# Grouped expert FFN: token parts of 8 (or 20 and 12) in place of 12 and 20, one slot array of 144 tiles, and slot tiles between the routing of later parts

## The chip, the cores and the metric

The kernel runs on one core of a Trainium2 chip. The metric is the device time of one execution in microseconds; lower is better. TensorE (PE) does the matrix products, VectorE (DVE) and ScalarE (ACT) the elementwise work, GpSimd (POOL) issues the indirect DMAs, SyncE (SP) the plain ones. All data are float32.

## The reference

The input is 8 sequences of 512 tokens with 256 features, 4096 token rows in all. Two layers run one after the other, each with a half-weighted FFN, an attention and another half-weighted FFN, and each of these reads a layer-normalized x:

```python
x = x + 0.5 * L0_ffn(LN(x))      # 8 experts, each takes its top k tokens
x = x + L0_attn(LN(x))           # rope, causal, 16 heads of 16
x = x + 0.5 * L0_ffn(LN(x))
x = x + 0.5 * L1_ffn(LN(x))      # mixture of experts, the first one
x = x + L1_attn(LN(x))           # 16 heads of 64; adds its input as well
x = x + 0.5 * L1_ffn(LN(x))      # the second one
```

The change concerns `L1_ffn`. Each token chooses 4 of 16 experts:

```python
scores = softmax(x @ gate_w.T)                  # 16 experts in 4 groups of 4
masked = scores of the 2 groups with the largest maximum, 0 elsewhere
weights, indices = top_k(masked, 4)
a = silu(x @ w1[e]) * (x @ w3[e])               # 256 -> 128, for each chosen e
y = sum over the chosen e of weight * (a @ w2[e])
z = (silu(x @ ws1) * (x @ ws3)) @ ws2           # shared expert, 256 -> 256 -> 256
return y + z
```

## The kernel before

**Stages.** x stays in SBUF as 32 token tiles of 128 rows. In the profiled execution the stages follow each other like this: first FFN of layer 0 (`ffn0(0)`) to about 660 us, its attention (`attn0`) to 1466, `ffn0(1)` to 2116, the first mixture-of-experts stage (`ffn1_before`) to 2670, the attention of layer 1 (`attn1`) to 3979, and the second mixture-of-experts stage (`ffn1_after`) to the end at 4489.

**Slots.** The mixture of experts is grouped. A token row goes to DRAM four times, once for each of its experts, into rows ("slots") ordered by expert, so that each slot tile of 128 rows belongs to one expert; the tiles are then multiplied by that expert's weights, and the results are gathered back. `Grouped` holds this for one stage. The 32 token tiles are cut into two parts, `PARTS = 12, 20`; the first stage takes them as (12, 20), the second as (20, 12). Each part has its own slot arrays in DRAM, `slots_d[t]` for the inputs and `ys_d[t]` for the outputs. Every expert's rows are rounded up to whole tiles, so that a part of t token tiles needs

```python
return (t * P * TOPK + E1 * (P - 1)) // P      # 63 for t = 12, 95 for t = 20
```

slot tiles, 158 for a stage, whatever the tokens choose. Slots that no token takes must hold finite numbers; `clear` (L133 to L135) writes zeros to `slots_d`, 20.2 MB in 16 DMAs on SP, from inside the expert loop of `ffn0(0)`.

**Steps of a part.**
- *Rows and logits.* Statistics (bn at L157 and L158, finish at L165 to L173), normalized rows (`rows`, L1212), transposes (`columns`, L1409 and L1412), router products (`logits`, L1417) into a PSUM tile `lg` that holds the part's token tiles.
- *Routing* (`routing`, L1244 to L1321). A generator of short groups of DVE operations, advanced from outside: softmax, four rounds of top-k (L1177 to L1188), a prefix sum over the tokens by expert with two matmuls (`pp`, L1282 and L1290), the slot number of each choice (`pick`, `where`, L1305 to L1309), the expert of each slot tile (`owner`, L1317), the weights of the choices (`coef`).
- *Sends* (`send`, L1221). Four indirect DMAs for each token tile, issued on POOL. A manual dependency keeps two of them in flight.
- *Slot tiles* (`tile_steps`). For each group of four tiles a load `xs` (L1488, on SP; it waits for all sends of its part) and a store `ys` (L1538). One tile is: transposes `tpx` (L1500), a `value_load` of the expert's number on PE (L1503), four matmuls `hs` (L1510), silu and product (L1516, L1518), transpose `tpa` (L1522), two matmuls `yps` (L1530). The stages of five successive tiles are interleaved in one `step`.
- *Collecting* (`collect`). One step adds the four results of token tile t-2 to x (L1341, DVE) and issues four gathers of token tile t (L1328, POOL), into two `yg` buffers.

**Order.** In both stages the order on PE, DVE, ACT, POOL and SP is the program's (`manual_schedule` with these engines); in `ffn0` SP is not in that list, in `attn0` neither POOL nor SP. The shared expert is cut into units of PE work with the DVE work that follows; `Pump` issues the PE part of the next unit and then the DVE part of the last one (hidden L1438 to L1449, outputs L1460 and L1466).

In `ffn1_before` all preparation comes ahead of the slot tiles: rows and routing of part 0, its sends, rows, logits and routing of part 1, its sends, with shared units between; then 158 tiles in one row. From tile 69 on, every sixth step is followed by one collecting step of part 0. `attn1` takes the collecting steps of part 1 over, 22 of them, one with each second half-chunk, prepares the first part of the second stage on the side (`Front`: rows on POOL, router products, `routing(0)`), and sends its rows (`front.send`). In `ffn1_after` the tiles of part 0 (20 token tiles) start at once, the routing of part 1 is advanced by two with every step, and its sends follow. After the last tile comes the shared expert of all 32 token tiles, with the remaining collecting steps between the units; each token tile is stored when its collected rows and its shared outputs are in (L1743).

Of the kernel before, what the change touches and what calls it, by code (L numbers as in the profile page):

```python
# [46 lines left out]
PARTS = 12, 20  # L47
# [9 lines left out]


def slot_tiles(t):

    return (t * P * TOPK + E1 * (P - 1)) // P


class Kernel:
    def __init__(self, ctx, tc, w):
# [59 lines left out]
        self.slots_d, self.ys_d = {}, {}  # L125
        for t in PARTS:
            self.slots_d[t] = self.dram.tile([slot_tiles(t) * P, D], F32, name=f"slots_d{t}")
            self.ys_d[t] = self.dram.tile([slot_tiles(t) * P, D], F32, name=f"ys_d{t}")

    def clear(self, zero, part, parts):  # L130

        for t in PARTS:
            rows = self.slots_d[t].rearrange("(j p) d -> p j d", p=P)  # L133
            a, b = slot_tiles(t) * part // parts, slot_tiles(t) * (part + 1) // parts
            self.nc.sync.dma_start(out=rows[:, a:b, :], in_=bc(zero, 1, b - a))  # L135
# [69 lines left out]
    def _ffn0(self, ctx, n, beside):  # L205
# [272 lines left out]
        if n == 0:  # L478
            zero = pool.tile([P, D], F32, name="zero")
            nc.gpsimd.memset(zero, 0.0)  # L480
# [5 lines left out]
        for e in range(E0):  # L486
# [4 lines left out]
            if n == 0:  # L491
                self.clear(zero, e, E0)
# [40 lines left out]
    def _attn0(self, ctx, weights):  # L533
# [330 lines left out]
        with tc.manual_schedule(engines={E.PE, E.DVE, E.Activation}):  # L864
# [22 lines left out]
            for g in range(G):  # L887
                n, kt = divmod(g, QT)
                b, half = divmod(g // 8, 2)
                if g % 8 == 0:  # L890
                    units = (first_half, second_half)[half](b)
                    if half == 1 and b + 2 < B:
                        normal(b + 2)()
                if g < 8:
# [39 lines left out]
    def _attn1(self, ctx, weights, beside, after):  # L934
# [172 lines left out]
        steps = after.routing(0, front.lg, front.pool, row_psum)  # L1107
# [14 lines left out]
        with tc.manual_schedule(engines={mybir.EngineType.PE, mybir.EngineType.Pool}):  # L1122
# [5 lines left out]
            for n in range(N):  # L1128
# [10 lines left out]
                for half in range(2):  # L1139
# [6 lines left out]
                    if half == 0 and n > 0 and beside:  # L1146
                        beside.pop(0)(behind)
# [43 lines left out]
class Grouped:  # L1191


    def __init__(self, k, n, parts):
        self.k, self.n, self.parts = k, n, parts
        self.base = (0, parts[0])
        self.tiles = [slot_tiles(t) for t in parts]
        self.slots_d = [k.slots_d[t] for t in parts]
        self.ys_d = [k.ys_d[t] for t in parts]
        late, most = k.late, max(parts)  # L1200

        self.slot = [late.tile([P, TOPK, most], I32, name=f"slot{h}", bufs=2) for h in range(2)]
        self.coef = [late.tile([P, TOPK, most], F32, name=f"coef{h}", bufs=2) for h in range(2)]

        self.owner = [late.tile([1, slot_tiles(most)], I32, name=f"owner{h}") for h in range(2)]
        self.stats = k.ln_tiles(late)
        self.sent, self.of_part = [], ([], [])
        self.got, self.y = [], {}

# [6 lines left out]
    def send(self, h, t, row):  # L1216

        nc, tc = self.k.nc, self.k.tc
        key = f"slots{self.n}{h}"
        for r in range(TOPK):  # L1220
            inst = nc.gpsimd.indirect_dma_start(  # L1221
                out=self.slots_d[h][:, :],
                out_offset=bass.IndirectOffsetOnAxis(ap=self.slot[h][:, r, t : t + 1], axis=0),
                in_=row, in_offset=None,
                bounds_check=self.tiles[h] * P - 1, oob_is_err=True,
# [4 lines left out]
            tc.declare_no_dep(inst, group=key, keep=before, reason="slots of one part are all different")  # L1230
            tc.add_to_no_dep_group(key, inst)
# [3 lines left out]
    def routing(self, h, lg, pool, row_psum):  # L1235
# [40 lines left out]

# [6 lines left out]
        inc = pool.tile([P, E1, HT], F32, name=f"left{E1}")  # L1283
        nc.vector.tensor_tensor_scan(inc.rearrange(flat), carry.rearrange(flat), pb, 0.0, ALU.mult, ALU.add)
        tiles_i = pool.tile([P, E1], I32, name="tiles_i")
        nc.vector.tensor_scalar(tiles_i, inc[:, :, HT - 1], float(P - 1), None, ALU.add)
        nc.vector.tensor_scalar(tiles_i, tiles_i, 7, None, ALU.arith_shift_right)
        nc.vector.tensor_tensor(inc.rearrange(flat), inc.rearrange(flat), pb, ALU.subtract)
        pa = row_psum(E1 * HT)
        nc.tensor.matmul(pa, lhsT=k.tri, rhs=chosen.rearrange(flat), start=True, stop=True)  # L1290
        tiles = pool.tile([P, E1], F32, name="tiles")
        nc.vector.tensor_copy(tiles, tiles_i)
        upto = pool.tile([P, E1], F32, name="upto")
        nc.vector.tensor_tensor_scan(upto, k.ones[:, 0:E1], tiles, 0.0, ALU.mult, ALU.add)
        base = pool.tile([P, E1], F32, name="base")
        nc.vector.tensor_tensor(base, upto, tiles, ALU.subtract)
        nc.vector.tensor_scalar(base, base, float(P), None, ALU.mult)
        nc.vector.tensor_tensor(inc.rearrange(flat), inc.rearrange(flat), pa, ALU.add)
        yield
        nc.vector.tensor_tensor(inc, inc, bc(base, 2, HT), ALU.add)  # L1300
        yield
        where = pool.tile([P, TOPK, HT], F32, name="where")
        for r in range(0, TOPK, 2):
            pick = pool.tile([P, 2, HT, E1], F32, name="pick")
            nc.vector.tensor_tensor(  # L1305
                pick, hots[:, r : r + 2], bc(inc.rearrange("p e t -> p t e"), 1, 2), ALU.mult
            )
            nc.vector.tensor_reduce(where[:, r : r + 2], pick, AX.X, ALU.add)
        nc.vector.tensor_copy(self.slot[h][:, :, :HT], where)  # L1309
        yield  # L1310

        past = pool.tile([P, E1], F32, name="past")
        number = pool.tile([P, 1], F32, name="number")
        nc.vector.tensor_scalar(past, upto, k.lanes[:, 0:1], None, ALU.is_le, ALU.add, accum_out=number)  # L1314
# [265 lines left out]
def ffn1_before(k, f):  # L1580
# [3 lines left out]
    with ExitStack() as ctx, k.tc.manual_schedule(engines={E.PE, E.DVE, E.Activation, E.Pool, E.SP}):  # L1584
# [76 lines left out]
        for late in coming:  # L1661
            late()
# [220 lines left out]
```

## Time and profile before

| | |
|---|---|
| time, median of 3 runs | 4433.28 us (4429.19 to 4433.55) |
| the profiled execution: time, span | 4490.85 us, 4489.1 us |
| mean granted TensorE clock in it | 0.918 of full |
| PE busy | 3938.8 us, 88% of the span |
| DVE, ACT, POOL busy | 1951.8, 1451.5, 1224.7 us |
| first mixture-of-experts stage | 2116 to 2670 us; first slot tile's `hs` at 2318.4, last `yps` at 2669.3 |
| second one | 3979 to 4489 us; slot tiles from 4000.5 to 4354.2 |
| slot tiles in both stages | 316 |
| sends (L1221) of the first stage | 48 from 2177.7 to 2243, 80 from 2289.5 to 2440 |

The profile comes from one execution, whose time stands in the table beside its span; the median comes from other executions of the same kernel. Rows of stretches give the busy time of each engine between two points of the span, the number of instructions in brackets, the granted clock of TensorE as a share of full speed, the mean busy share of the 16 DMA engines and what they moved. Rows of a chain give start, length, engine, output tile and line of what the end waited for. Rows of a line give the shortest, median and longest duration in ns, and the first and last start.

### The profile page before, as it was taken

The numbers are of one execution on the slowest core, as the hardware profiler recorded it, in microseconds if no ns is written. First come the engines' busy times: TensorE is split into PE (matmuls) and PEld (weight loads), VectorE is DVE, ScalarE is ACT, GpSimd is POOL, SyncE is SP. The second block draws the span as 40 slices with busy tenths as digits, with TensorE's granted clock in tenths as the row PEclk, the third lists the DMA queues.
The fourth block names the chain that finished last, engine by engine and source line by source line (L and its number), as shares of the span: only waits on it lengthen the run. The fifth ranks groups of instructions, "written<-read, shape, count | busy, mean of one in ns | idle before, by whom it ended". The sixth has DMA issues, their size and how long they took to land.

```text
span 4489.1 us, 52262 instructions
## 1 busy us (share of the span) xinstructions
PE 3938.8 (88%) x17900; PEld 2336.3 (52%) x17900; DVE 1951.8 (43%) x4992; ACT 1451.5 (32%) x3289; POOL 1224.7 (27%) x1133
## 2 busy tenths in 40 slices
PE   5799988999999579998679889999999999989987
PEld 5466653333334556665446654545554554556654
DVE  5221115545454422111443445666555455454454
ACT  2122222433343212222113324454445434433321
POOL 2323323333230132332433212231000112524145
PEclk9999997989896589999789999999999999989998
DMA  8423320000000322332325530010000000135443
GB/s 276 139 58 65 72 58 19 15 20 13 22 22 3 95 55 56 66 72 61 114 81 181 182 116 24 24 33 15 1 1 1 1 1 20 57 116 177 150 149 106
DMA packets 253715, 306.99 MB, mean 68 GB/s; under 512 B 31888, under 2 KB 223504, under 8 KB 253200
## 3 DMA queue, kind: packets, MB, share of 16 engines
q1 hardware_dynamic: 204304, 202.42, 14.7%
q0 software_dynamic: 49152, 101.24, 9.3%
q8 instruction: 148, 2.42, 0.2%
q14 instruction: 111, 0.91, 0.1%
HBM read 161.48 MB, written 133.69 MB: 66 GB/s over the span
## 4 chain that ended last, share of the span: by engine, by line
PE 58%; DVE 11%; issue 6%; ACT 5%; DMA 2%; another core or an unknown queue 1%; POOL 1%; SPq 0%; DVEq 0%; ACTq 0%; POOLq 0%
PE hs L1510 7%; PE pq L1001 5%; PE zp L1061 5%; PE sp L1027 5%; PE op L464 5%; PE hp L453 4%; PE tp L1048 4%; PE st L775 3%; PE yp L1091 3%; PE pv L982 2%; PE pp L643 2%; PE hp L1438 2%; PE yps L1530 2%; ACT ex L1036 1%; DVE x L1341 1%
## 5 line engine op out<-in xcount | busy, mean ns | idle before, releaser
L1036 ACT ACTIVATE ex<-sp,nmax 128x512 f32<-128x512 f32 x512 | 347.4, 689 | 415.7 <-DVE nmax L1033 381.8
L464 PE MATMUL op<-w,hid 128*128 128x256 f32 x2048 | 473.2, 394 | 0.0
L453 PE MATMUL hp<-exT,w 128*128 128x512 f32 x1024 | 448.4, 596 | 0.0
L464 PEld LDWEIGHTS op<-w,hid 128*128 128x128 f32 x2048 | 405.9, 199 | 66.9 <-issue 8.6
L1510 PE MATMUL hs<-w_sb,xT 128*128 x1264 | 363.1, 411 | 74.1 <-DVE xT L195 59.2
L1328 POOL DMA_INDIRECT yg<-ys_d,slot x256 | 262.5, 1025 | 599.5 <-DVE x L1341 249.8
L471 POOL DMA_INDIRECT acc_d<-ob,idx x128 | 199.7, 1560 | 693.4 <-ACT ob L470 396.4
L469 DVE TENSOR_TENSOR ob<-op,b 128x256 f32<-128x256 f32 x128 | 54.4, 425 | 663.7 <-PE op L464 573.7
L1033 DVE TENSOR_REDUCE nmax<-sp 128x2 f32<-128x1024 f32 x256 | 303.3, 1217 | 72.1 <-PE sp L1027 70.6
L1510 PEld LDWEIGHTS hs<-w_sb,xT 128*128 128x128 f32 x1264 | 221.7, 193 | 204.7 <-DVE xT L195 115.8
L1048 PEld LDWEIGHTS tp<-ident,ex 128*128 128x128 f32 x2048 | 227.3, 141 | 190.8 <-issue 129.0
L453 PEld LDWEIGHTS hp<-exT,w 128*128 128x128 f32 x1024 | 194.8, 192 | 232.8 <-issue 231.9
L1048 PE MATMUL tp<-ident,ex 128*128 128x128 f32 x2048 | 275.7, 278 | 36.4 <-ACT eT L193 35.9
L746 DVE CUSTOM_DVE_ANT_0 junk<-sp,mask 128x128 f32<-128x128 f32 (+3 forms) x512 | 248.4, 485 | 126.1 <-PE sp L739 106.6
L457 ACT ACTIVATE hid<-hp,b 128x512 f32<-128x512 f32 x256 | 175.9, 687 | 343.4 <-PE hp L453 340.3
L1027 PE MATMUL sp<-qk,qk 64*128 64x512 f32 x1024 | 262.9, 633 | 1.9 <-ACT ex L1036 1.9
L1221 POOL DMA_INDIRECT slots_d<-wide,slot x176 | 173.7, 987 | 331.7 <-DVE past L1314 125.5
L1001 PE MATMUL pq<-xnT,wide 128*128 128x512 f32 x512 | 252.4, 616 | 6.3 <-DVE eT L195 5.6
L784 ACT ACTIVATE ex<-st 128x1024 f32<-128x1024 f32 (+3 forms) x256 | 174.0, 703 | 239.3 <-DVE st L782 239.0
L1518 DVE TENSOR_TENSOR as<-sgs,hs 128x128 f32<-128x128 f32 x316 | 90.5, 286 | 363.3 <-ACT sgs L1516 330.4
L1061 PE MATMUL zp<-eT,v 128*64 128x512 f32 x1024 | 235.8, 602 | 0.3 <-DVE eT L195 0.3
L470 ACT ACTIVATE ob<-ob,gate 128x256 f32<-128x256 f32 x128 | 65.0, 508 | 510.3 <-DVE ob L469 480.0
(293 smaller groups left out, 6087.2 us busy)
## 6 DMA issues: line engine op xcount, KB each, us to landing
xs<-slots_d SPq DMA_DIRECT2D x76, 512.0 KB
ys_d<-ys SPq DMA_DIRECT2D x76, 512.0 KB
w<-in_W SPq DMA_DIRECT2D x32, 1024.0 KB
w_sb<-in_w SPq DMA_DIRECT2D x24, 512.0 KB
slots_d<-zero SPq DMA_DIRECT2D x7, 1536.0 KB
xn_d<-xn SPq DMA_DIRECT2D x16, 512.0 KB
acc_d<-x SPq DMA_DIRECT2D x8, 1024.0 KB
x<-acc_d SPq DMA_DIRECT2D x16, 512.0 KB
```

The costliest lines, as they stand in the source:

```text
L453: nc.tensor.matmul(hp, lhsT=w1[:, c, f * P : f * P + P], rhs=exT[e][:, c, h * CH : h * CH + CH], start=(c == 0), stop=(c == DC - 1),)
L464: nc.tensor.matmul(op, lhsT=hid[h][:, f, i * P : i * P + P], rhs=w2[:, f, :], start=(f == 0), stop=(f == FC - 1),)
L471: nc.gpsimd.indirect_dma_start(out=acc_d[:, :], out_offset=bass.IndirectOffsetOnAxis(ap=idx[:, e, st : st + 1], axis=0), in_=ob, in_offset ...
L746: nc.vector.tensor_tensor_reduce(out=junk[:, :wd], in0=sps[h // 2][:, h % 2, :wd], in1=mask[:, S - wd :], scale=1.0, scalar=NEG, op0=ALU.a ...
L1001: nc.tensor.matmul(pp, lhsT=(wq, wk)[a][:, k, c * P : c * P + P], rhs=seq[b]["xnT"][:, k, :], start=(k == 0), stop=(k == DC - 1),)
L1027: nc.tensor.matmul(sp[:, j, :], lhsT=q[r, qt * P : qt * P + P], rhs=k[r, :], start=True, stop=True)
L1033: latest[0] = nc.vector.tensor_reduce(nmax, sp, AX.X, ALU.max, negate=True).ins
L1036: nc.scalar.activation(ex[:, j, :], sp[:, j, :], AF.Exp, bias=nmax[:, j : j + 1], accum_out=ch["sums"][:, qt, j : j + 1],)
L1048: nc.tensor.transpose(tp[:, k, :], ch["ex", qt][:, j, k * P : k * P + P], self.ident)
L1061: nc.tensor.matmul(zp[DK1 * j : DK1 * j + DK1, :], lhsT=seq[b]["v", h][:, k, at : at + DK1], rhs=ch["eT"][:, j, k, :], start=(k == 0), sto ...
L1328: inst = nc.gpsimd.indirect_dma_start(out=y[:, r, :], out_offset=None, in_=self.ys_d[h][:, :], in_offset=bass.IndirectOffsetOnAxis(ap=self ...
L1510: nc.tensor.matmul(hp.rearrange("p a i -> p (a i)"), lhsT=st[j]["xT"][:, c, :], rhs=self.w13[:, bass.ds(st[j]["e"], 1), c, :].rearrange("p ...
```

## The change

The slots of a stage now lie in one array for all parts, `SLOTS = FULL + E1 = 128 + 16 = 144` tiles, with one `slots_d` and one `ys_d` in DRAM. Of each expert's rows in a part, as many as fill whole tiles take tiles numbered upwards from the last part's end. What is left over goes to shared tiles, one for each expert at first, numbered downwards from 143, which later parts go on filling; when one is full, the next one downwards is begun. `routing` carries this from part to part in `free`, `rest`, `ends` and `ended`. Tiles from 128 up have a fixed expert (`SLOTS - 1 - number`), so PE loads no number for them.

The constructor works out an order of tiles that holds for any choice of the tokens: `closed[h]` tiles can be computed once the parts before h are sent, and after `ready[h]` tiles everything of part h is computed. For four parts of 8 token tiles `closed` is [0, 17, 33, 49] and `ready` [65, 96, 144, 144]; for parts of 20 and 12, [0, 65] and [96, 144].

```diff
-PARTS = 12, 20
+FULL = TT * TOPK
+SLOTS = FULL + E1
...
     def clear(self, zero, part, parts):
-        for t in PARTS:
-            rows = self.slots_d[t].rearrange("(j p) d -> p j d", p=P)
-            a, b = slot_tiles(t) * part // parts, slot_tiles(t) * (part + 1) // parts
+        a, b = SLOTS * part // parts, SLOTS * (part + 1) // parts
+        for rows in (self.slots_d, self.ys_d):
+            rows = rows.rearrange("(j p) d -> p j d", p=P)
             self.nc.sync.dma_start(out=rows[:, a:b, :], in_=bc(zero, 1, b - a))
...
-            if n == 0:
-                self.clear(zero, e, E0)
...
+                if g >= 16 and g % 8 == 0 and g < 16 + 8 * B:
+                    self.clear(mask[:, 0:D], g // 8 - 2, B)
```

The last two hunks are in the expert loop of `ffn0` and in the step loop of `attn0`; `ys_d` is now cleared too, 37.7 MB together.

In `routing` the rounding to whole tiles gives way to the split into whole tiles and left-over rows; the new operations work mostly on 16 numbers a partition, a few on all (128 for 8 token tiles). `then()` stands for the sends of the part, which are now issued as soon as `slot` is written:

```diff
+        nc.vector.tensor_scalar(over_i, count, P - 1, None, ALU.bitwise_and)
+        nc.vector.tensor_scalar(count, count, 7, None, ALU.arith_shift_right)
+        nc.vector.tensor_copy(tiles, count)
+        nc.vector.tensor_copy(over, over_i)
...
+        full = small("full")
+        first = 0.0 if h == 0 else self.ends[:, 0:1]
+        nc.vector.tensor_tensor_scan(full, k.ones[:, 0:E1], tiles, first, ALU.mult, ALU.add)
...
+        if h > 0:
+            limit, jump, more, other = small("limit2"), small("jump2"), small("more"), small("other")
+            nc.vector.tensor_tensor(limit, jumps[0][0], self.free, ALU.add)
+            nc.vector.tensor_tensor(more, over, self.free, ALU.is_ge)
...
+            jumps.append((limit, jump))
+            yield
+        beyond = [pool.tile([P, E1, HT], F32, name=x) for x in ("masked", "score2")[: len(jumps)]]
+        for b, (limit, jump) in zip(beyond, jumps):
+            nc.vector.tensor_tensor(b, at, bc(limit, 2, HT), ALU.is_ge)
+            nc.vector.tensor_tensor(b, b, bc(jump, 2, HT), ALU.mult)
...
-        nc.vector.tensor_copy(self.slot[h][:, :, :HT], where)
+        nc.vector.tensor_copy(self.slot[:, :, ts], where)
+        then()
```

The rows, columns, logits (now copied from a PSUM tile of four token tiles to SBUF) and the routing of part h are one generator, `front(h)`. `ffn1_before` becomes:

```diff
+        part = f.front(0)
+        while 0 not in f.lg:
+            advance(part, 1)
+        advance(part, 4)
+        pump.feed(groups[0][0] + groups[1][0] + groups[0][1])
+        while advance(part, 3):
             pump.run(1)
...
+        part = f.front(2)
+        while 2 not in f.lg:
+            advance(part, 3)
+            pump.run(1)
+        advance(part, 4)
+        pump.feed(groups[2][1] + groups[4][0])
+        tiles(f.closed[1], part, 3)
...
+        part = f.front(3)
+        pump.feed(groups[3][1] + groups[5][0] + groups[4][1])
+        tiles(f.closed[2], part, 3)
...
+        tiles(f.closed[3], iter(()), 1)
         while pump.units or pump.pending:
             pump.run(1)
-        coming = f.collect(0, 2)
-        begin, weights = f.tiles[0] + 6, None
-        for i in range(total):
+        coming = f.collect(2)
+        begin, weights = f.ready[0] + 6, None
+        for i in range(at, total):
             step(i)
...
-            if i >= begin and (i - begin) % 6 == 0 and coming:
+            if i >= begin and len(coming) > (TT + 2 - f.base[2]) * TOPK:
                 coming.pop(0)()
```

`tiles(until, work, each)` issues one `step` and then advances `work` by `each`. So tiles 0 to 16 run beside the routing of part 2, tiles 17 to 32 beside the rows and routing of part 3, tiles 33 to 48 after it, the other 95 behind the last shared units.

Collecting goes in quarter steps: one add of token tile t-2 and one gather of token tile t for one of the four choices. In the first stage one quarter step follows each tile from tile 71 on; 72 quarter steps are left to `attn1`, which takes four at a time. In `ffn1_after` one or two of them follow each tile from tile 102 on, now with four gathers in flight from the start, and three, three, one, one, one, one follow the shared units after the tiles. Loads of `xs` now wait for the sends of their own and all earlier parts, gathers for the stores of the tiles up to `ready` of their part. A group of loads has at most four tiles and does not reach across a `ready` mark; one group has a single tile.

## The prediction

> **What bounds the kernel now.** I read the head of the page first, then busy time by stretches for the two mixture-of-experts (MoE) stages that the diff rewrites (2116 to 2670 us and 3979 to 4489 us), then the chain of waits inside them, then single lines of code.
>
> ```profile
> PE 3938.8 (88%) x17900; PEld 2336.3 (52%) x17900; DVE 1951.8 (43%) x4992; ACT 1451.5 (32%) x3289; POOL 1224.7 (27%) x1133
> PE   5799988999999579998679889999999999989987
> PEclk9999997989896589999789999999999999989998
> ```
>
> PE is busy 88% of the span, so overall there is little to win except by doing less on PE or by closing the dips. The first MoE stage is digits 19 to 24 of the second and third rows, the second one the last five. The stretches show where its dips are:
>
> ```profile
> core 0: us, PE busy (x) PEld busy (x) DVE busy (x) ACT busy (x) POOL busy (x), PEclk, DMA share, GB/s
> 2142.00:2181.00 39.00, 32.11 (x71) 15.13 (x71) 26.89 (x80) 6.98 (x10) 2.64 (x3) 0.79 0.36 98
> 2181.00:2250.00 69.00, 37.17 (x171) 28.67 (x169) 23.66 (x83) 10.66 (x17) 44.49 (x46) 0.73 0.27 103
> 2250.00:2316.00 66.00, 54.05 (x150) 29.87 (x151) 43.69 (x96) 6.53 (x10) 19.30 (x19) 0.89 0.09 36
> 2316.00:2344.00 28.00, 18.21 (x70) 12.52 (x69) 6.43 (x20) 5.17 (x18) 17.68 (x19) 0.82 0.36 120
> 2344.00:2470.00 126.00, 116.51 (x553) 83.21 (x554) 46.34 (x154) 44.32 (x153) 44.17 (x45) 1.00 0.58 183
> ```
>
> The row of 2344 is the goal: slot tiles back to back, PE busy for 116.5 of 126 us at full granted clock. Everything from 2142 to 2316 is preparation: routing of part 0, rows of part 1, routing of part 1, with the shared expert as the only filler. PE is busy 123 of 174 us there, at a clock of 0.73 to 0.89. No slot tile runs before 2318. One tile's price is read in the chain of waits:
>
> ```profile
> 2460.98 1.15 PE hs L1510 x4
> ...
> 2471.28 1.13 PE hs L1510 x4
> ...
> 2473.50 10.88 DMA xs<-slots_d
> ```
>
> From 2460.98 to 2471.28 are five tiles: 2.06 us each (2.04 over 2344 to 2352). Then the tiles of part 0 are over and PE waits 10.9 us for part 1's rows. The second MoE stage has tiles from 4000.5 to 4354.2 (158, 2.24 us each, with routing or collecting between them), then a tail without tiles:
>
> ```profile
> 4214.00:4354.00 140.00, 117.64 (x557) 84.10 (x557) 70.00 (x208) 45.39 (x156) 58.14 (x58) 1.00 0.52 163
> 4354.00:4404.00 50.00, 38.83 (x99) 20.61 (x98) 20.55 (x44) 5.41 (x10) 32.78 (x31) 0.83 0.33 94
> 4404.00:4489.00 85.00, 61.39 (x200) 36.30 (x198) 38.47 (x82) 9.86 (x17) 41.22 (x40) 0.90 0.38 113
> ```
>
> ```profile
> 4369.39 2.95 DMA yg<-ys_d,slot
> 4372.43 0.49 DVE x L1341
> 4373.08 0.67 POOL yg L1328
> ```
>
> The tail's chain goes round POOL gather, transfer, DVE add, next gather: 71 gathers and 76 adds in 131 us, about 1.8 us per gather. PE has about 100 us of work there.
>
> **The change part by part.**
>
> *Fewer tiles.* 158 slot tiles become 144 in each MoE stage. Fourteen tiles by 2.05 us is 29 us less in each, and it is on the path, since tiles follow each other on PE. In the second stage 16 shared tiles also lose their value_load; 0 to 4 us, taken as 0, since the row of 2344 already has PE 92% busy.
>
> *First stage, order of work.* A timeline. Logits of 8 rather than 12 token tiles: from 2142 to about 2138. Routing of 12 token tiles takes 23.4 us of DVE in 70 instructions, of 20 tiles 32.7 us; the line through both gives 18.7 us for 8. The diff adds 14 small operations to the first routing (about 3 us at 0.2 us) and some 26 to each later one, part of them on all 128 elements (5 to 6 us). All routing together grows from 56 to about 95 us of DVE. That is the change's main price. Part 0's slots are then known at about 2166 (2176.7 before); rows and logits of part 1 until 2190; its routing until 2227; rows of part 2 until 2246, all with shared-expert units on PE. Then 17 whole tiles run beside part 2's routing: 24 us of routing plus 17 by 0.75 us of the tiles' own DVE work is 37 us of DVE in short dependent steps, so I put a step at 3.0 us instead of 2.05: until 2298. Shared units, 10 us. Sixteen tiles beside part 3's rows and routing: 9.5 (1.18 us a token tile, from the 23.66 us of 20 in the row of 2181) +24+12 = 46 us of DVE, 3.6 us a step: 2366. Shared units 14 us (2380), 16 tiles at 2.05 (2413), the last shared units 25 us (2438). The remaining 95 tiles carry 64 quarter steps of collecting; before, a tile with a quarter step cost 2.3 us (2.24 in the second stage with routing), so 95 by 2.05 plus 64 by 0.25 is 211 us: 2649. If the interleaved steps cost only 2.3 us, as the second stage's mixed steps do at their cheapest, 33 us less: 2616. I take 2634, nearer the dear end, because DVE has twice the routing work; 36 us before the 2670 of now. Check from below: 144 tiles, 82 us of shared units (3.44 and 0.86 us each), 36 us of transposes and logits, 22 us until the first logits and 16 of collecting add to 450 us, so 2566 is the floor.
>
> *The sends.* Now 128 row transfers go out from inside the routing (L1221), beside tiles. Their instructions:
>
> ```profile
> L1221 POOL DMA_INDIRECT slots_d<-wide,slot x48: 975/979/1032, 2177.7 to 2242.4; - x48
> ...
> L1221 POOL DMA_INDIRECT slots_d<-wide,slot x45: 974/979/988, 2340.2 to 2438.9; - x45
> ```
>
> The first row has no slot tiles beside it (1.35 us a send), the second has tile loads and stores (2.2 us a send, two in flight). 32 sends at 2.1 us are 67 us: part 0 done at 2230, part 1 at 2290, part 2 by 2355, part 3 from 2364 to 2431. Each is there before its tiles are due, with 0 to 15 us to spare (part 3's at 2438). Here a rule speaks against the change: the Trainium skill, "SBUF — State Buffer", section "SBUF: two separate sides", says that a POOL-issued DMA cannot have its descriptors written while VectorE holds the port they share (620 ns becoming 3100 ns there), so sends inside DVE-heavy routing should slow. The trace says otherwise for these shapes: 974 to 988 ns with DVE at 46 of 126 us, 979 median beside the 24 of 69 us. At the trace's price sends stay hidden; if each of the 96 sends beside routing cost 2.5 us more, 240 us of POOL would make part 3 arrive over 150 us late and take all the gain. I follow the trace.
>
> *Wait at 2473.* Its 10.9 us go if part 3 is in time; late next would be the end of the sends at 2431. This is within the timeline.
>
> *Clearing.* ffn0(0) loses 20.2 MB of DMA writes; the DMA share was 1.05 there, and from indices ready to first hidden matmul took 18.3 us against 14.5 in ffn0(1): 4 us less. The second array adds 16.8 MB more: 37.7 MB now issued on SP in attn0 at every eighth step, 16 transfers. At the 335 to 357 GB/s of the first stage that is about 107 us of DMA; attn0's own traffic there is 0.12 of the share. A pair (4.7 MB, 14 us) delays q and k loads queued behind it on SP by 14 us, while these are asked for 6 to 8 steps (42 to 48 us) ahead. So 0, between 0 and +80.
>
> *attn1.* It takes over 72 quarter steps (18 whole ones) instead of 22 whole: 4 by 4 adds of 0.48 us is 8 us of DVE less, 3 us more routing, on an engine 57% busy under a PE of 96% (2700 to 3950 us): 0, within 5 either way.
>
> *Second stage.* 29 us less for tiles; routing of 12 token tiles 5 us longer, in steps of 2.2 to 3.3 us: +5; a group of one tile and rows that arrive about when due: +2. Sum −22. In the tail 65 gathers are left instead of 71, at 1.8 us each 11 us less, in quarter steps with four in flight rather than in fours; PE's 100 us stand below. I take −12 (between −30 and +10, since the chain shows 9.5 us of bare issue at 4437 there, which no row explains).
>
> Sum: −4 +0 −36 +0 −22 −12 = −74 us. The profiled execution is 4490.85 us (span 4489.1, 1.75 around it), 1.3% above the median 4433.28; 4417/4490.85 of the median is 4360. Its own range: 4330 to 4390.
>
> **The rivals.**
> - *All hidden* (0.15): interleaved tiles cost 2.05 to 2.3, the tail falls by 25. First stage −58, second −27−25, −4: −114, so 4320. For it: DVE is 43% busy. Against: routing is a dependent chain of 0.5 us operations in one in-order queue with the tiles' evictions.
> - *Sends bound the end* (0.22): at 2.3 us each the 128 sends run from 2166 without a break and end at 2461; the last 95 tiles stand until then, 2461+211 = 2672, and the first stage gains nothing: −4−22−12, 4395. For it: only 7 us of slack in my timeline. A hold-up like the one in the chain at 2225 ("another core or an unknown queue", 21.18) would make it 4416.
> - *Clear in front of q and k, slower* (0.09): SP is idle from 670 to 698 us and, in attn0, not ordered by hand. If the 16 transfers are issued in one burst before the first q and k loads at 698, those land 75 to 85 us late, and attn0 stands. It turns the sign as soon as the delay is over 74 us; price 80+, result about 4440 to 4448.
> - *Gain not there* (0.04): DVE steps of 4.5 us in the interleaved stretch (+45) and no tail gain: about 4415 to 4430.
>
> **How the numbers follow.** Likeliest 0.50. What this kernel's measurement can tell from no change is about 0.2%, 9 us. Faster 0.86 (first three, most of the last), same 0.04, slower 0.10. Range from just under "all hidden" to the edge of "gain not there": 4310 to 4428; the clear case and some of the best are outside.
>
> **What would show it.** 144 tiles of tpx per stage, tiles beginning near 2246 rather than 2318; their steps at 3 to 3.6 us during routing; no wait for xs at the last part; end of the stage near 2634; tile phase of the second stage some 320 us long; DMA share of ffn0(0) lower at 65 to 143; attn0 still about 806 us long. I am wrong if sends take over 1.1 us of POOL, if PE waits for L1488's loads, or if attn0 grows.

## The result: 0.7% faster where 1.7% was forecast

The changed kernel takes 4407.62 us in the median of 11 runs, the kernel before 4433.70 us: a ratio of 0.9933, 95% interval 0.9918 to 0.9949. One of the 11 took 13575.9 us and is left out of the ratio. The gain is 26 us by the medians, not 74. The time lies inside the range of the forecast, but that range reached to within 6 us of the kernel before, so this says little for the forecast.

The profiled execution of the changed kernel is an ordinary one (4405.38 us, span 4403.7 us, clock 0.916). The one shown of before (4490.85 us) was not: it is 57 us above the median, and those 57 us turn out to be the main thing (see the next section). The head of the page after:

```profile
PE 3892.5 (88%) x17660; PEld 2305.1 (52%) x17660; DVE 1966.9 (45%) x5201; ACT 1437.6 (33%) x3226; POOL 1225.5 (28%) x1132
PE   5799987999999769999678988999999999998988
PEclk9999997889996579999689999999999999998999
```

PE is busy 46 us less than in the profile shown of before. The first mixture-of-experts stage by stretches, after:

```profile
core 0: us, PE busy (x) PEld busy (x) DVE busy (x) ACT busy (x) POOL busy (x), PEclk, DMA share, GB/s
2142.00:2181.00 39.00, 24.85 (x62) 12.70 (x62) 28.45 (x111) 5.31 (x8) 5.34 (x6) 0.72 0.42 117
2181.00:2250.00 69.00, 47.51 (x152) 31.41 (x152) 39.22 (x154) 12.88 (x19) 44.23 (x45) 0.67 0.29 101
2250.00:2316.00 66.00, 50.30 (x207) 34.37 (x208) 44.40 (x175) 18.71 (x52) 37.40 (x39) 0.93 0.41 134
2316.00:2344.00 28.00, 24.10 (x111) 18.71 (x110) 14.98 (x58) 10.09 (x25) 8.39 (x9) 0.82 0.38 123
2344.00:2470.00 126.00, 112.63 (x469) 77.57 (x468) 54.10 (x178) 30.40 (x98) 31.42 (x32) 0.96 0.34 109
```

Against the rows shown of before this looks like success: tiles run from 2250 on, and PE is busy for 122 of the 163 us from 2181 to 2344, where it was 109. But the kernel before was profiled again later, on another chip, in an execution of 4421.04 us (b_fourth below). The same stretches of it:

```profile
2142.00:2181.00 39.00, 27.37 (x71) 14.43 (x70) 33.04 (x103) 3.88 (x6) 11.48 (x12) 0.82 0.09 38
2181.00:2250.00 69.00, 54.01 (x220) 35.30 (x218) 44.99 (x116) 13.68 (x21) 35.84 (x37) 0.90 0.22 86
2250.00:2316.00 66.00, 60.59 (x240) 40.12 (x241) 25.00 (x68) 14.89 (x47) 39.16 (x40) 0.96 0.38 134
2316.00:2344.00 28.00, 26.03 (x126) 18.48 (x124) 10.40 (x35) 9.81 (x34) 11.56 (x12) 1.00 0.55 174
2344.00:2470.00 126.00, 111.05 (x517) 78.96 (x518) 46.95 (x152) 41.80 (x143) 42.63 (x44) 0.99 0.60 200
```

Here the old kernel is busier on PE than the new one in every stretch up to 2344, at a higher clock. It enters the stage at 2115.6 us, 15 us before the changed kernel (2130.4), so the same times are not quite the same work; with its stretches set 15 us earlier PE is still busier in each of the four (32.8, 56.8, 53.0 and 25.8 us). Its first slot tile's matmul starts 163 us after its stage does, not 191 as in the profile shown of before. Much of the idle time in the preparation that the forecast set out to fill was not there.

The tail after:

```profile
4300.00:4350.00 50.00, 45.14 (x135) 24.11 (x133) 26.17 (x58) 7.00 (x13) 37.98 (x38) 0.97 0.42 118
4350.00:4404.00 54.00, 44.88 (x158) 27.06 (x156) 26.77 (x59) 7.40 (x13) 29.90 (x29) 1.00 0.47 143
```

The stages of these executions, with their borders taken from the first and last matmuls of each (us). "Usual" is the change from b_fourth to a_fourth (the changed kernel on the same chip), except that for attn0 the means of all profiles stand: 808 us in nine without clears in it, 821 in eleven with them.

| stage | before, as shown | b_fourth | after | a_fourth | usual | forecast |
|---|---|---|---|---|---|---|
| ffn0(0) | 672.9 | 671.5 | 667.8 | 666.6 | -5 | -4 |
| attn0 | 810.6 | 800.0 | 817.3 | 827.4 | +13 | 0 |
| ffn0(1) | 644.2 | 644.1 | 645.3 | 645.1 | +1 | 0 |
| first MoE stage | 541.6 | 505.1 | 517.6 | 515.5 | +10 | -36 |
| attn1, with its start | 1331.2 | 1327.3 | 1328.8 | 1328.3 | +1 | 0 |
| second stage, tiles | 353.8 | 349.8 | 321.0 | 320.4 | -29 | -22 |
| second stage, tail | 134.9 | 121.6 | 105.9 | 105.4 | -16 | -12 |
| sum | | | | | -25 | -74 |

### The profile page after: what moved, and what is told of

It is laid out like the page before. It is cut to its first block, busy times and chain, and to the rows that moved or that the text cites. A ratio compares the mean times of both kernels' runs of the same rounds, so it can differ in the third digit from the quotient of the medians.

```text
span 4403.7 us, 51503 instructions
## 1 busy us (share of the span) xinstructions
PE 3892.5 (88%) x17660; PEld 2305.1 (52%) x17660; DVE 1966.9 (45%) x5201; ACT 1437.6 (33%) x3226; POOL 1225.5 (28%) x1132
## 4 chain that ended last, share of the span: by engine, by line
PE 35%; DVE 7%; issue 4%; DMA 3%; ACT 3%; POOL 1%; SPq 0%; POOLq 0%; DVEq 0%; ACTq 0%
PE pq L992 5%; PE hs L1651 5%; PE sp L1018 5%; PE zp L1052 5%; PE tp L1039 4%; PE pv L973 3%; PE yp L1082 2%; DMA yg<-ys_d,slot 2%; ACT ex L1027 2%; DVE nmax L1024 1%; PE hp L1571 1%; POOL yg L1424 1%; PE yps L1671 1%; DMA acc_d<-ob,idx 1%; DVE xT L189 1%
## 5 line engine op out<-in xcount | busy, mean ns | idle before, releaser
L1651 PE MATMUL hs<-w_sb,xT 128*128 (+1 forms) x1152 | 338.5, 418 | 54.6 <-DVE xT L189 46.0
L1651 PEld LDWEIGHTS hs<-w_sb,xT 128*128 128x128 f32 x1152 | 205.7, 198 | 175.7 <-DVE xT L189 96.4
L1059 POOL COPY wide<-rec 128x512 f32<-128x512 f32 x64 | 39.3, 614 | 672.5 <-PE rp L1065 577.2
```

The lines of the kernel that those rows point to most:

```text
L1651: nc.tensor.matmul(hp.rearrange("p a i -> p (a i)"), lhsT=st[j]["xT"][:, c, :], rhs=self.w13[:, st[j]["e"], c, :].rearrange("p e i -> p (e ...
```

## The experiments

They ran on five chips, each experiment beside the kernel before on the same chip. A ratio is always to that. Each chip was used on one occasion, so "chip" below stands for the chip and its occasion.

**The same two kernels again.** No edit in b_again and a_again.

> The kernel before, unchanged, for a second profile. Theory: the profiled execution of before (4490.85 us) was a slow one, 57 us above the median of the timed runs, and its two mixture-of-experts stages or its attention stages hold stretches that an ordinary execution does not have; a second profile should then read 4425 to 4445 us, with the 57 us gone from places that can be named (the hold-ups at 2225 and 4437 us, the wait at 2473, or attn0). Rival: the profile is ordinary and recording it costs this kernel 57 us; then a second one reads 4480 to 4495 with the same stage times within 5 us. Timed ratio to before 1.000 either way.

> The changed kernel, unchanged. Theory and rival alike: 4395 to 4413 us, timed ratio 0.993 to 0.995. It tells how far stage times differ from one execution to the next: if attn0 (803 us in the first profile of before, 809 in the one of after) moves by 10 us or more between two profiles of the same kernel, differences of that size between kernels are not of the change.

Measured on this chip: the kernel before 4487.05 us (67 runs), b_again 4494.8 us, ratio 1.0004 (0.9984 to 1.0025); the changed kernel 4494.83 us, ratio 1.0011 (0.9998 to 1.0024). The rival's time is right and its reason isn't: all runs of the kernel before on this chip are as slow, and on the fifth chip the profiled execution (4421.04 us) is no slower than the others (median 4433.22 us). So it is the chip, not one execution and not the recording. b_again's stages are within 5 us of the first profile's. On this chip the change gains nothing.

What goes with it is seen when TensorE's semaphore records are set beside the ends of the matmuls that raise it (a semaphore is the counter by which one engine tells another that it is done). In the first profile of the changed kernel none of 4207 such signals comes over 1.5 us late. In the profile shown of before 38 do, up to 11.8 us late, in b_again 31, in a_again 68. These counts depend on how a record is matched to its matmul; a stricter matching gives up to half as many again where there are any, and still none where there is none. VectorE and ScalarE have late signals in the same profiles. All of these late TensorE signals lie within 3 us of the start of an indirect DMA on POOL, though such times are only 40 to 45% of the span (29% in b_one). In the chain of waits they stand as rows without a releaser; of the kernel before as first shown:

```profile
2214.16 6.64 another core or an unknown queue
...
2225.07 21.18 another core or an unknown queue
```

and of a_again:

```profile
2209.79 4.02 another core or an unknown queue
2216.38 10.81 another core or an unknown queue x2
2265.20 8.82 another core or an unknown queue
```

The chain of b_fourth from 2150 to 2290 has no such row. The two rows of the first profile are 27.8 us by themselves.

**Interleaving and clears, first look.** a_seq runs all four routings ahead of the tiles:

```diff
-        tiles(f.closed[1], part, 3)
-        while advance(part, 1):
-            pass
-        pump.run(len(pump.units))
+        while advance(part, 3):
+            pump.run(1)
         part = f.front(3)
...
-        tiles(f.closed[3], iter(()), 1)
```

> The changed kernel with the first stage's interleaving undone: all four routings first, with shared-expert units as filler, then all 144 tiles in a row. Theory (running tiles beside routing hides about 20 us): tiles start near 2355 us after four routings, 144 by 2.05 plus 16 of collecting end at 2666 instead of 2648, so +15 to +22 us on the median. Rival (interleaved steps are so slow that nothing is gained by them): within 5 us of the changed kernel.

Ratio 1.0030 (1.0015 to 1.0044), 4503.15 us: 8 us more than a_again, just clear of the noise. Interleaving is worth something, less than expected.

a_clear takes the clears back into ffn0(0):

```diff
+            if n == 0:
+                self.clear(zero, e, E0)
...
-                if g >= 16 and g % 8 == 0 and g < 16 + 8 * B:
-                    self.clear(mask[:, 0:D], g // 8 - 2, B)
```

> The changed kernel with both arrays cleared in the expert loop of ffn0(0), as before (37.7 MB there), and nothing cleared in attn0. Theory (the clears cost attn0 nothing; ffn0(0) gained 5 us by losing them): +5 to +12 us, since the writes there are now nearly twice as many as in before. Rival (the clears in attn0 hold up q and k loads and took back part of the gain): attn0 shorter by 8 us or more and the whole 5 to 20 us faster than the changed kernel.

Ratio 0.9998 (0.9984 to 1.0011), 4487.91 us: 7 us less than a_again, again only just clear of the noise. In the profiles ffn0(0) is 6.2 us longer, attn0 16.5 us shorter. Single profiles give attn0 only to some 10 us: it is 800 to 811 us in the four of the kernel before and 817 to 827 in the four of the changed one. The size is the rival's; its mechanism is tested below.

**Is the rate of POOL's DMAs the cause?** On a second chip, again with late signals:

> The kernel before, unchanged. Theory: its profile of 4490.85 us holds delays that come from the chip and not from the program. In that profile and in the second one, completion signals of TensorE's matmuls (its semaphore 110) are seen 1.5 to 12 us late in 23 to 26 places, nearly all while POOL issues indirect DMAs back to back; in the first profile of the changed kernel no signal is late. If these runs are on a chip without late signals: 4425 to 4445 us, no late signal, first stage 20 us or more shorter and tail 20 us or more shorter than in the first profile. If on one with them: 4480 to 4495 again. Rival: the 57 us lie in the attentions, as granted clock.

> The changed kernel, unchanged, beside the kernel before on the same chip. Without late signals: 4400 to 4412 us, ratio 0.993 to 0.995. With late signals: 4485 to 4500 us, ratio 0.999 to 1.003, the first stage 15 to 20 us longer than before's and the second stage some 30 us shorter. Rival (the two ratios so far differ by chance): any ratio between, and no relation to late signals in its profile.

b_third 4509.94 us with 54 late signals, a_third 4506.75 us with 71; ratio of the changed kernel 0.9982 (0.9956 to 1.0007). Stages from b_third to a_third: first stage +20, tiles of the second -12, tail -6 us.

```diff
-            before = self.sent[-2:-1]
+            before = self.sent[-1:]
```

> The changed kernel with one send in flight instead of two (before = self.sent[-1:]), in all stages. Theory (POOL issuing sends back to back delays TensorE's signals): on a chip with late signals the first stage is 15 to 25 us shorter than the changed kernel's and 5 or fewer late signals are left between 2170 and 2450 us; on a chip without them it is 3 to 10 us longer, since 32 sends at 2.5 us end later. Rival (the delay has nothing to do with the rate of sends): 3 to 10 us longer on either chip.

Ratio 1.0365 (1.0311 to 1.0419), 4687.04 us. Both texts missed the time by far. With one in flight the sends start 2.97 us apart (103 of them from 2176.3 to 2479.0), the first stage is 48 us longer than a_third's, and in attn1 and the tiles of the second stage all waited too (+62 and +50 us). The theory's count came true: in the first stage no late TensorE signal is left, where a_third has 18; the 48 that the profile still has lie in ffn0 and the second stage. Sends one at a time do away with the late signals there, and cost more than these do.

```diff
-        coming = f.collect(4, done)
+        coming = f.collect(2, done)
```

> The changed kernel with two gathers in flight in the second stage instead of four. Theory as before, for gathers: on a chip with late signals the tiles and the tail of the second stage (339 and 124 us in a_again) become 8 to 20 us shorter together; on a chip without (321 and 106) they become 5 to 12 us longer. Rival (four in flight is simply better): 5 to 12 us longer on either.

Ratio 0.9990 (0.9965 to 1.0016), an interval that takes in a_third's ratio; the median of 4521.37 us is 15 us above a_third's. Late TensorE signals went from 71 to 36 in all, and in the second stage, which alone is edited, from 37 to 1. Yet its tiles and tail took 3 and 5 us more, as the rival has it. So fewer transfers in flight remove the late signals here too and bought no time. Whether the slower collecting cost as much as they did, or such a chip costs something besides late TensorE signals, no run tells.

**Without most of the transfers.** A third chip, with late signals too.

```diff
-        for r in range(TOPK):
+        for r in range(1):
             inst = nc.gpsimd.indirect_dma_start(
...
-            x, self.y[t][:, r, :], self.coef[:, r, t : t + 1], x, ALU.mult, ALU.add
+            x, self.y[t][:, 0, :], self.coef[:, r, t : t + 1], x, ALU.mult, ALU.add
```

> The kernel before with one of the four sends and one of the four gathers of each token tile in both mixture-of-experts stages (the other three are left out; the four adds stay and read the first gather's rows). It takes three quarters of POOL's indirect DMAs out of these stages. Theory (those DMAs delay the other engines' signals on this kind of chip): no more than a third of the late TensorE signals of before are left in the two stages, and the time falls by 50 to 90 us. Rival (they cost only where something waits for a transfer: 11 us at 2473, some 25 in the tail): 30 to 40 us.

> The changed kernel with the same three of four sends and gathers left out. Theory (the change saves 55 to 75 us of TensorE and waiting time, and POOL's DMAs took it back through late signals): 55 to 80 us below b_one. Rival (the longer routing and the slower interleaved steps take back what 28 tiles save, with or without transfers): 10 to 35 us below b_one.

b_one 4414.67 us, ratio 0.9845 (0.9824 to 0.9866), 73 us less than before. 13 late signals are left, 5 of them in the two stages, where b_again has 19: time and count are the theory's. Its first stage is 506.0 us, 35 us less than b_again's and as long as b_fourth's with all transfers. What leaving them out is worth without late signals was not run. a_one 4382.16 us, ratio 0.9766 (0.9746 to 0.9786): 32.5 us below b_one. That is the rival's answer: with the transfers out of the way the change still gains only about 30 us, and its first stage gains 1 us (505.0). The missing gain was not taken by the transfers.

**The tiles alone.**

```diff
+        self.done = [{63: 57, 95: 87}[t] for t in self.tiles]
...
-        where = [(h, j) for h in range(2) for j in range(self.tiles[h])]
+        where = [(h, j) for h in range(2) for j in range(self.done[h])]
```

> The kernel before with 144 tiles computed in each mixture-of-experts stage, and nothing else of the change: the last 6 tiles of the part of 12 and the last 8 of the part of 20 are left out (their results are read as zeros), and the collecting steps come every fifth and third tile instead of every sixth and fourth, so that as many as before are in the tile loops. It is the tile term of the prediction alone: 28 by 2.05 = 57 us less than before. Rival (tiles are partly filled by collecting steps that now stand closer): 30 to 45 us less.

Ratio 0.9917 (0.9896 to 0.9938), 4448.93 us, 39 us less than before on that chip; the profile has 24 us less in each stage than b_again, and 4 us more in the tail. The rival was right on the size: 1.7 us of a stage for a tile; its reason, that the same number of collecting steps lies between fewer tiles, is likely and not tested by itself. So 28 fewer tiles bring 39 us there, while the whole change came out between 8 us slower and 15 us faster by the medians on chips of that kind. Taken together, everything else in it costs there.

a_whole gathers the quarter steps into whole ones at the same rate:

```diff
-                for _ in range(1 + i % 2):
-                    coming.pop(0)()
+                debt += 1 + i % 2
+                if debt >= TOPK:
+                    debt -= TOPK
+                    for _ in range(TOPK):
+                        coming.pop(0)()
```

> The changed kernel with the second stage's collecting in whole steps of four adds and four gathers at the same mean rate as its quarter steps. Theory (quarter steps keep POOL and DVE going evenly): 5 to 15 us longer than the changed kernel (median 4495 and 4507 us on two chips, ratio 1.001 and 0.998 to before), most of it in the tail. Rival (no difference, only four in flight counts): within 4 us of it.

Ratio 1.0000 (0.9986 to 1.0014); tail 124.5 us, a_again's is 123.9. No effect of quarter steps is to be seen on a chip with late signals; on one without it wasn't tried.

**What costs.** A fourth chip, without late signals: the kernel before 4433.32 us.

> a_one with the first stage's interleaving undone as in a_seq: four routings first, then 144 tiles (three of four sends and gathers still left out). Theory (four routings are the price, interleaving neither helps nor hurts much): first stage 500 to 512 us as in a_one (505), time within 8 us of a_one's ratio 0.977. Rival (interleaved steps are dear, 2.9 us a tile instead of 2.05): first stage 480 to 495 us and a ratio of 0.971 to 0.974. Third (interleaving hides routing): 520 us or more, ratio over 0.980.

a_seq_one (a_one with a_seq's edit) has a first stage of 524.9 us, a_one 505.0: the third text. Interleaving hides 20 us, if a_one's chip with its few late signals may stand beside this one. Its ratio, 0.9913 (0.9898 to 0.9929), can't be set beside a_one's, since the kernel before is faster here. Four routings in front of the tiles are dear even without transfers.

b_clear makes a_clear's edit the other way round, in the kernel before.

> The kernel before with the clears taken out of ffn0(0) and put into attn0 as in the changed kernel, both kinds of arrays (the 12 and 20 ones of inputs and results, 158 tiles each, 41 MB). Theory (they make attn0 longer by half-clock time, no load waits): ffn0 4 to 5 us shorter, attn0 8 to 15 us longer than the 805 to 811 us of before, in all +3 to +10 us. Rival (attn0's length is chance): attn0 within 5 us of 808, in all -4 us.

Ratio 1.0030 (1.0017 to 1.0043), 14 us slower, more than the theory's most. ffn0(0) is 3.6 us shorter than in b_fourth, attn0 is 827.5 us. The stretch of attn0, b_fourth:

```profile
671.50:1471.50 800.00, 712.29 (x4053) 306.88 (x4054) 422.06 (x1548) 293.65 (x492) 222.68 (x191) 0.84 0.08 23
```

and b_clear:

```profile
667.90:1495.40 827.50, 740.99 (x4052) 314.23 (x4053) 422.28 (x1546) 293.45 (x492) 222.54 (x190) 0.81 0.23 72
```

Same instructions, same busy time on DVE, ACT and POOL; the DMA share rises from 0.08 to 0.23, the granted clock falls from 0.84 to 0.81, and PE's busy time grows by 29 us, the stage by 27.5. (b_fourth's attn0 is the shortest of all; b_clear's is 19 us above the mean of the nine profiles without clears.) In attn0 of the first profile after, PE's idle time ahead of the score matmuls (L728) and their weight loads that ended on a q or k load is 0.8 us: the stage does not wait for loads. Time at half clock in attn0 is 250 to 278 us in the nine profiles without clears, 298 to 325 in ten with them, and 257 in one with them (a_seq, 803.5 us). That the clears lengthen attn0 is shown by this edit and a_clear, and that it goes with more time at half clock by the profiles; by what path they lower the clock isn't shown.

**Two parts instead of four.** a_two keeps the 144 tiles and the second stage, and cuts the first stage into two parts of 16 token tiles. All routing (still `front(h)`) and all shared units come ahead of the tiles, as in the kernel before, and it clears in ffn0(0). So three things differ from the changed kernel: the parts, the interleaving (dropping it alone cost time in a_seq and a_seq_one) and the place of the clears.

```diff
-        one = Grouped(k, 0, (8, 8, 8, 8))
+        one = Grouped(k, 0, (16, 16))
```

> The changed kernel with two parts of 16 token tiles in the first stage, all routing ahead of the tiles with shared units as filler, and both arrays cleared in ffn0(0); 144 tiles and the second stage as in the changed kernel. Theory (the tiles' 39 us are kept where routing isn't cut into four, and attn0 keeps its 810 us): first stage 515 to 530 us against 541 to 561 of before on such a chip, ratio to before 0.988 to 0.993, so better than the changed kernel (1.001 and 0.998). Rival (sends of 64 rows in a burst and late signals take it as well): ratio 0.997 or more.

Ratio 0.9912 (0.9897 to 0.9926), 4394.97 us, first stage 490.7 us. From its last tile to attn1 it takes 11.9 us instead of 7.8, because collecting runs up to the last tile and the first rows of attn1 wait for it in the chain, and attn1 is 10 us longer. Against a_two, a_two_b leaves three more groups of steps to attn1:

```diff
-            if i >= begin and len(coming) > (TT + 2 - f.base[1]) * TOPK:
+            if i >= begin and len(coming) > (TT + 2 - f.base[1] + 3) * TOPK:
```

On a fifth chip, without late signals:

> The kernel before, unchanged. On a chip without late signals: 4425 to 4445 us, and its profile has a first stage of 505 to 512 us instead of 541.6, tiles of the second stage at 350, a tail of 120 to 124 instead of 134.9, attn0 at 805 to 811 us. On one with late signals: 4480 to 4520 with stages as in b_again. Rival to the first: a first stage of 530 us or more without a late signal.

> The changed kernel, unchanged, for a comparison on one chip. Without late signals: ratio 0.993 to 0.995, first stage 515 to 520 us, attn0 815 to 830. With: ratio 0.998 to 1.003, first stage 555 to 585.

> a_two with three collecting steps of four more left to attn1, so that none stands at the end of the first stage's tiles. Theory (four parts are the step that failed): ratio to before 0.988 to 0.992, 8 to 20 us below a_fourth on either kind of chip, first stage 485 to 495 us without late signals. Rival (a_two was better by its clears alone): within 6 us of a_fourth less 12.

b_fourth 4433.22 us; first stage 505.1, tail 121.6, no late signal. a_fourth 4406.26 us, ratio 0.9927 (0.9912 to 0.9942). a_two_b 4377.23 us, ratio 0.9872 (0.9856 to 0.9888): it beats both, the changed kernel by 29 us on the same chip, more than the theory's 8 to 20 and too much for the clears alone. Its first stage is 486.6 us and its attn0 806.9, against 515.5 and 827.4. The first stage of a_two_b:

```profile
2200.00:2280.00 80.00, 57.13 (x199) 35.87 (x200) 50.88 (x157) 12.56 (x19) 57.06 (x57) 0.78 0.26 92
2280.00:2340.00 60.00, 55.14 (x227) 37.12 (x226) 19.87 (x56) 13.90 (x44) 33.79 (x35) 0.99 0.44 146
2340.00:2470.00 130.00, 117.39 (x556) 83.17 (x555) 46.48 (x155) 44.69 (x154) 31.28 (x32) 1.00 0.50 159
```

From 2280 on PE runs at full clock with nothing but tiles and the last shared units, while in the changed kernel the stretch of 2344 still has the rest of the preparation in it at 0.96.

## Why the prediction was wrong, step by step

**The step that failed: the base of the first stage, "36 us before the 2670 of now".** The timeline of the changed kernel was good: first tile forecast at 2246, measured 2250.5; tiles again after the shared units at 2308, 2380 and 2438, measured 2304.7, 2382.6 and 2438.9; end at 2649 by its dear end (2634 was taken), about 2648 measured. What was wrong is what it was subtracted from. The stage took 541.6 us in the profile shown and takes 505.1 in an execution like the timed ones: 36.5 us of it, as much as the forecast gain, belong to an execution with late signals: 27.8 us stand in the chain as the two rows without a releaser, and b_one has a stage of 506.0 us on such a chip once most transfers are gone. The forecast quoted the row of 21.18 us ("another core or an unknown queue") and put it into a rival, but left it in the base. The term missed by 46 us (-36 forecast, +10 measured): these 36.5, and some 10 because the stage ended near the dear end of its timeline, not at 2634.

**Scaling by the ratio of the times.** The forecast knew that its profile was 1.3% above the median and spread that over everything. The difference was not spread: of the 70 us between that profile and b_fourth's, 36 lie in the first stage, 13 in the tail, 11 in attn0, 4 in the tiles of the second stage and 4 in attn1. Most of it is in the places that the diff rewrites.

**The price of routing** was sized well and underrated in effect. DVE's routing work in the first stage goes from 56.1 to 92.7 us (forecast: 56 to 95). The chain of waits of the changed kernel in the interleaved stretch shows who sets the step there:

```profile
2258.70 0.30 DVE rank L1173
2259.03 0.30 DVE m L1176
2259.35 0.30 DVE hots L1177
2259.68 0.31 DVE left L1180
2260.49 0.34 DVE xT L189
2261.06 0.30 DVE rank L1173
```

Top-k (L1173 to L1180) and evictions (`xT`) stand in one queue, and PE waits. In b_fourth the 49th tile begins 261.5 us after the stage, in the first profile of the changed kernel 308.5: 47 us later. From there it needs 209 us instead of 244. The difference is 12 us (10 in a_fourth). With two routings (a_two_b) this DVE work is 64.4 us, and the stage is 29 us shorter than a_fourth's.

**Fewer tiles**: right in kind. Alone, 39 instead of 57 us (b_144, on a chip with late signals); in the second stage, without them, tiles and all -29 where -22 was forecast.

**The sends**: POOL's time for one is as it was:

```profile
L1245 POOL DMA_INDIRECT slots_d<-wide,slot x128: 974/979/1390, 2173.9 to 2416.5; - x128
```

The rule of the Trainium skill ("SBUF — State Buffer", "SBUF: two separate sides") that was weighed against the change speaks of VectorE operations in a 2-port mode, a limit that the prediction left out. It was rightly set aside for the sends' own time: the median of the row above is the 979 ns of before. Part 3's rows were there at about 2419, before the 2438.9 that needs them.

**The clears, "so 0, between 0 and +80"**: the term was mis-sized. The forecast looked for loads that wait and found none; the clock was not in its list of costs. b_clear puts 14 us on the move with ffn0(0)'s gain in it, so some 18 on attn0; the means of the profiles say 13. The forecast had named a longer attn0 as a sign of being wrong.

**The tail**: -12 forecast, -16 measured. POOL's idle time in it that ends on a DVE add or a gather falls from 21.8 us in b_fourth,

```profile
  DVE x L1341: 13.8, 10
...
  DMA yg<-ys_d,slot: 8.0, 14
```

to 2.3 us after:

```profile
  DVE x L1443: 1.7, 4
  DMA yg<-ys_d,slot: 0.6, 2
```

**attn1** was 0 and is +1. **ffn0(0)** was -4 and is -5.

Of the rivals none came true as written. "Clear in front of q and k" had the right sign of its term with the wrong mechanism and a size four times too large.

## What to carry to other kernels

If the profile's execution is slower than the timed runs, find the stage that holds the difference before any stage of it is used as a base; a row in the chain that no engine or queue explains is the first suspect, and a second profile of the unchanged kernel is the cheapest test. Filling idle PE time with other work pays only as long as the filler's own serial work does not grow: here cutting the routing into four more than doubled its instructions (140 to 367) in the queue that also carries the evictions, and with it cut into two, ahead of the same 144 tiles, the stage was 29 us shorter. A bulk transfer that nothing waits for can still cost (14 us in b_clear, at a lower granted clock); move it as an edit of its own first.

## What the runs showed of the hardware that was not expected

On three of the five chips, and in the profile first shown of before, TensorE's completion signals come up to 17 us late (b_third) close to indirect DMAs of POOL; on the others none is (0 of 4200 to 4299 in seven profiles, counting the first of the changed kernel). The DMAs themselves are no slower: a send's time on POOL has a median of 976 to 979 ns on both kinds. The kernel before takes 4487 to 4522 us on the one kind and 4433 on the other, the changed kernel 4495 to 4507 and 4406 to 4408, so the change's gain holds on one kind only. The late signals follow the number of these DMAs and how many are in flight: leaving out three quarters leaves 5 of 19 in the two stages (b_one), one send in flight leaves none of 18 in the first stage (a_pace), two gathers instead of four 1 of 37 in the second (a_fly2). Only the first, which leaves work out, was faster. What sets the two kinds of chip apart isn't settled.
